# B and C of a state pair computed back to back on two halves of the array, the spline's scale moved into its clamps, and the planner's preference set to zero

## The chip, the cores and the metric

The kernel runs on one core of one Trainium2 chip. The metric is the device time of one execution in microseconds (us); three executions of the kernel before gave a median of 16343.33 us. One further execution was recorded by the hardware profiler; all views below are of that one.

## The reference

The input x has 32 images of 128 channels and 56 x 56 pixels, float32. Four residual layers follow each other, each on a group-normalised copy (`_gn`, 32 groups of 4 channels):

```python
x = x + _L0_conv_ref(_gn(x), ...)   # 1x1 conv with weights mixed per image, three dilated depthwise convs, SiLU
x = x + _L1_conv_ref(_gn(x), ...)   # cubic B-spline of every element
x = x + _L2_conv_ref(_gn(x), ...)   # linear attention over pooled keys, then a 3x3 depthwise conv
x = x + _L3_conv_ref(_gn(x), ...)   # Mamba layer over 3136 tokens
```

Two parts matter here. The spline layer clips the normalised element to -2..2 and sums ten cubic B-splines over 14 equidistant knots, with coefficients `coeffs`. The Mamba layer has 256 inner channels and 16 states a channel, and runs a recurrence over the 3136 tokens of an image:

```python
dA = jnp.exp(delta[..., None] * A)
dBu = delta[..., None] * B_ssm[:, :, None, :] * xc[..., None]
def step(h, inp):
    dA_t, dBu_t, C_t = inp
    h = dA_t * h + dBu_t
    y = jnp.einsum('bdn,bn->bd', h, C_t)
    return (h, y)
```

`delta`, `B_ssm` and `C_ssm` are projections of the same tokens, so B and C have 16 rows each for every token, shared by all 256 channels.

## The kernel before

**Tiling.** An image lies in on-chip memory as 128 channels x 3136 pixels and is worked in 7 chunks of 448 (`CH`, 8 rows of pixels). In the Mamba layer, a chunk is a `Scan` of 16 steps (`STEPS`): 8 pairs of states (`NPAIR`) times 2 halves of the channels (`DI`). One step covers 2 states x 128 channels, as two blocks of 64 channels x 2 states. There are 32 x 7 x 16 = 3584 steps, and the rest of the network is arranged around them.

**One scan step `n` of pair `p = n // 2`.** `b_rows` (line 1069) spreads the two B rows of the pair over 128 partitions by a matmul with a 0/1 matrix `sel` into the tile `pb`, which comes from a PSUM pool of a single buffer (`ps_bc`). `c_rows` (line 1060) does the same for C into a tile `mm` of the shared PSUM pool `ps_mm` of three buffers, and ScalarE copies it to `cb` (three buffers). Both happen only at the first of a pair's two steps and go through `both` (line 1054): B lies on rows 0 to 63 of `dbl`, C on rows 64 to 127, each with its low half of the bits 32 rows further on, so each matmul has 64 rows. `decay` (line 1076) makes two `da` tiles by Exp on ScalarE, into PSUM. `state` (line 1084) multiplies `du` by `pb` on VectorE into `h` and runs two scans with `da` over it. `products` (line 1100) multiplies `h` by `cb` on GpSimd into `hc`. `add` (line 1108) sums `hc` into the PSUM tile `y` by matmuls.

**The other work.** Beside the scan of image b run `until_scan` of image b+1 (spline, attention, first normalisation) and `first_layer` of image b+2 (the dynamic conv). Both are Python generators, called piece by piece from `images` (line 1196) so that their instructions are spread over the steps. `ssm_inputs` and `gate` prepare the next chunk's `delta`, `du`, `dbl` and `sz`.

**The spline** (line 747). Four lanes of 32 partitions hold the same 32 channels, each lane with another knot. For a chunk, ScalarE makes 12 hats `|a u + b|` (Abs, with the column `scl` as scale and a column of `bia` as bias) and, for each of four groups of channels, one Relu over three hats, `1 - |.|`. TensorE then sums the hats with weights `wspl`; squares, cubes and additions follow on ScalarE, VectorE and GpSimd. `scl` is 3.25/std of the channel (13 intervals over 4), `bia` is made of the knot's number and the mean.

**The order.** Nothing is issued as it is written. Each call becomes a `Work` with an engine, a modelled cost (`price`), the regions it reads and writes, a step and a value `ahead`; `plan.issue` then puts all works of a loop body into one order, and each engine executes its part of it strictly in that order. `plan.at(g, FIRST)` gives scan work of step g an `ahead` of 8, `SECOND` gives the next chunk's inputs 4, the rest has 0. A work is due at `(step - ahead) * 4.5` us, or earlier if a successor needs it. `attempt` (line 245) takes works one after the other in modelled time, at most 12 steps ahead of the oldest open one (`WINDOW`), each when its inputs and a buffer are there. Which of an engine's candidates is taken is decided here:

```python
late = at - self.PATIENCE[e] * (w.ahead > 0)
if w.table and w.table != table:
    late += 0.6
key = (max(late, free[e]), w.due, i)
```

`at` is when the work could start and `free` when the engine is free. With `PATIENCE` at 0.5 us, a scan work that can start up to 0.5 us after the engine is free counts as startable now, and if it is due earlier than other work that is ready, the engine is left idle for it. `plan.together(share)` joins the calls of a block into one work that is not split; its cost is the sum divided by `share` plus 0.1 us.

**Who calls what.** In `images`, step g calls `b_rows` for g+2, `state` g, `decay` g+1, `products` g, `c_rows` for g+`AHEAD` (2), `add` for g-2 and `store` for g-3.

Of the kernel before, what the change touches and what calls it, by code (L numbers as in the profile page):

```python
# [12 lines left out]
F32 = mybir.dt.float32  # L13
F32R = mybir.dt.float32r
AF = mybir.ActivationFunctionType
ALU = mybir.AluOpType
AX = mybir.AxisListType

P = 128
# [3 lines left out]
CH = ROWS * W  # L23
# [8 lines left out]
G = 32  # L32
NG = P // G
# [9 lines left out]
NKNOT = 14  # L43
# [11 lines left out]
DI = 2  # L55
# [11 lines left out]
NB = DI * P // Q  # L67
NPAIR = NST // 2
STEPS = NPAIR * DI
AHEAD = 2  # L70
LAG = 3
FIRST, SECOND = 8, 4
READY = 12
# [20 lines left out]
class Plan:  # L94
# [7 lines left out]
    TABLE = 1.28  # L102
    NEVER = 1e18
    GATE, BUSY = 3.413, 1.27
    PATIENCE = {"tensor": 0.5, "scalar": 0.5, "gpsimd": 0.3, "vector": 0.1, "sync": 0.0}

    def __init__(self, nc, tc):
        self.nc, self.tc = nc, tc
# [254 lines left out]
def tile_conv_stack(ctx: ExitStack, tc: tile.TileContext, out: bass.AP, x: bass.AP, w: dict):  # L363
# [150 lines left out]
    for s, knots in enumerate(KNOTS):  # L514
        for k, m in enumerate(knots):
            rows = slice(G * k, G * k + G)
            nc.vector.memset(kneg[rows, s : s + 1], -float(m))
            for i, (f, s1) in enumerate(SUMS):
                if s1 == s and (f == 2 or m % 2 == f):
                    nc.vector.tensor_copy(cs[rows, i : i + 1], (qc if f == 2 else py_)[rows, m - 1 : m])  # L520
# [61 lines left out]
    def psum(cols=CH, rows=P):  # L582
        t = ps_mm.tile([P, 512], F32, tag="mm", name="mm")
        return t[:rows, :cols]
# [161 lines left out]

    def spline(xt, st):
        mg, rs, ve, _ = group_stats(st)
        ab = small.tile([P, 2], F32, tag="ab", name="ab")

        kpu = (NKNOT - 1) / (GMAX - GMIN)
        nc.vector.tensor_scalar_mul(ab[:, 0:1], rs[:], kpu)
        nc.vector.tensor_mul(ab[:, 1:2], mg[:], ab[:, 0:1])
        nc.vector.tensor_scalar(ab[:, 1:2], ab[:, 1:2], -1.0, -GMIN * kpu, ALU.mult, ALU.add)

        top = small.tile([P, 1], F32, tag="top", name="top")
        nc.vector.tensor_mul(top[:], ve[:], rs[:])
        nc.scalar.activation(top[:], top[:], AF.Identity, bias=mg[:, 0:1], scale=GMAX)
        pab = psum(2 * NG)
        for c in range(NG):  # L760
            for k in range(4):
                nc.tensor.matmul(
                    pab[G * k : G * k + G, 2 * c : 2 * c + 2],
                    ident[:, G * c : G * c + G],
                    ab[:],
                    start=True,
                    stop=True,
                    tile_position=(0, G * k),
                )
        pab = pab.rearrange("p (c t) -> p c t", t=2)  # L770
        scl = small.tile([P, NG], F32, tag="scl", name="scl")
        nc.vector.tensor_copy(scl[:].unsqueeze(2), pab[:, :, 0:1])
        bia = small.tile([P, NG, 3], F32, tag="bia", name="bia")
        nc.vector.tensor_add(
            bia[:], kneg[:].unsqueeze(1).to_broadcast([P, NG, 3]), pab[:, :, 1:2].to_broadcast([P, NG, 3])
        )

        def load_u(j):

            t = stk.tile([P, NG, ROWS * PW], F32, tag="stack", name="stack")  # L780
            with plan.together():
                for k in range(4):
                    for c in range(NG):
                        nc.sync.dma_start(
                            t[G * k : G * k + G, c, 0:CH], xt[G * c : G * c + G, j * CH : (j + 1) * CH]
                        )
            return t

        us = [load_u(0)]
        after = Stats(xt)  # L790
        yield 6.0
        for j in range(NCH):
            if j + 1 < NCH:
                us.append(load_u(j + 1))
            u = us[j]
            xs = xt[:, j * CH : (j + 1) * CH]
            hats = wide.tile([P, NG, 3, CH], F32, tag="wide", name="hats")
            for c in range(NG):
                for s in range(3):
                    nc.scalar.activation(  # L800
                        hats[:, c, s, :], u[:, c, 0:CH], AF.Abs, bias=bia[:, c, s : s + 1], scale=scl[:, c : c + 1]
                    )
                nc.scalar.activation(hats[:, c], hats[:, c], AF.Relu, bias=one[:, 0:1], scale=-1.0)
                yield 3.6
            ind = tmp.tile([P, CH], F32, tag="v", name="ind")
            nc.gpsimd.tensor_scalar(ind[:], xs, top[:, 0:1], clast, ALU.is_ge, ALU.mult)

            def combined(f):
                ps = psum()
                mine = [i for i, (f1, _) in enumerate(SUMS) if f1 == f]  # L810
                for i in mine:
                    with plan.together(NG):
                        for c in range(NG):
                            nc.tensor.matmul(
                                ps[G * c : G * c + G, :],
                                wspl[:, i, :],
                                hats[:, c, SUMS[i][1], :],
                                start=(i == mine[0]),
                                stop=(i == mine[-1]),
                                tile_position=(0, G * c),  # L820
                            )
                return ps

            ps = combined(2)
            nc.vector.tensor_add(xs, xs, ps)
            nc.gpsimd.tensor_add(xs, xs, ind[:])
            after.take(j)
            yield 2.2
            for f in range(2):
                ps = combined(f)  # L830
                sq = tmp.tile([P, CH], F32, tag="v", name="sq")
                nc.scalar.activation(sq[:], ps, AF.Square)
                cube = tmp.tile([P, CH], F32, tag="v", name="cube")
                nc.vector.tensor_mul(cube[:], sq[:], ps)
                nc.gpsimd.tensor_add(xs, xs, cube[:])
                yield 1.7
        after.take(NCH)
        return after.st
# [202 lines left out]
    class Scan:  # L1041
# [15 lines left out]
            pair = sel[rows, 2 * p : 2 * p + 2, :].rearrange("p a b -> p (a b)")  # L1057
            nc.tensor.matmul(ps, pair, self.dbl[rows, :], start=True, stop=True)

        def c_rows(self, n):  # L1060

            p, db = divmod(n, DI)
            if db == 0:
                ps = psum()
                self.both(ps, C_ROW, p)
                self.cbs[p] = cbp.tile([P, CH], F32, tag="cb", name="cb")
                nc.scalar.copy(self.cbs[p][:], ps)

        def b_rows(self, n):

            p, db = divmod(n, DI)
            if db == 0:
                self.pbs[p] = ps_bc.tile([P, 512], F32, tag="bc", name="pb")[:, :CH]
                self.both(self.pbs[p], B_ROW, p)

        def decay(self, n):
            p, db = divmod(n, DI)
# [118 lines left out]
    def images(first, count, ahead):  # L1196
# [11 lines left out]
        def at(g, what):  # L1208

            if 0 <= g < count * NCH * STEPS:  # L1210
                getattr(scans[g // STEPS], what)(g % STEPS)
# [3 lines left out]
        for b in range(count):  # L1215
# [5 lines left out]
            for j in range(NCH):  # L1221
                k = b * NCH + j
                if k == 0:
                    last = new_last()
                    scans[0] = Scan(xt, image(ov, 0), last, 0)
                    for n in range(AHEAD):
                        at(n, "c_rows")
                    for n in range(2):
                        at(n, "b_rows")
                    at(0, "decay")  # L1230
                following = None
                if j + 1 < NCH:
# [5 lines left out]
                for n in range(STEPS):  # L1238
                    g = k * STEPS + n
                    plan.at(g)  # L1240
                    if n == 0 and j == NCH - 1:
                        rest.finish()
                    if n == READY:

                        following.finish()
                        gates.finish()
                        if j == NCH - 1:
                            layer0.finish()
                        if k + 1 < count * NCH:
                            nb, nj = divmod(k + 1, NCH)  # L1250
                            if nj == 0:
                                last = new_last()
                            scans[k + 1] = Scan(xts[nb % 3], image(ov, nb), last, k + 1)
                    plan.at(g, FIRST)
                    at(g + 2, "b_rows")
                    at(g, "state")
                    at(g + 1, "decay")
                    at(g, "products")
                    at(g + AHEAD, "c_rows")
                    at(g - LAG + 1, "add")  # L1260
                    at(g - LAG, "store")
                    plan.at(g, SECOND)
                    following.step(n)
                    if n >= READY - DI:
                        gates.step(n - READY + DI)
                    plan.at(g)
                    rest.step(j * STEPS + n)
                    if j * STEPS + n > LAG:
                        layer0.step(j * STEPS + n)
# [119 lines left out]
```

## Time and profile before

| what | value |
|---|---|
| three executions, us | 16294.26, 16343.33, 16363.43 |
| profiled execution: its own time, us | 16316.11 |
| profiled execution: span from first to last instruction, us | 16314.3 |
| mean granted TensorE clock, share of full speed | 0.893 |
| B matmul `pb<-dbl,sel`: count, mean ns | 1792, 512 |
| C matmul `mm<-dbl,sel`: count, mean ns | 1792, 502 |
| copy of C on ScalarE, `cb<-mm`: count, mean ns | 1792, 527 |
| decay `da`: count, mean ns | 7168, 633 |
| scan `h<-da,last,h`: count, mean ns | 6144, 1135 |
| `hc<-h,cb` on GpSimd: count, mean ns | 3584, 2092 |

How to read it: a busy time is the time in which an engine had an instruction in work; TensorE's are lengthened by its pipeline, so that the ends of two matmuls that follow each other overlap. An engine's idle time is put down to the instruction that released it last. All operations carry the line of a helper (338), which is why groups are told apart by the names of their tiles. The first 420 us are a prologue without a scan step; the last 400 us hold the scan of the last image alone, with the inputs of its own chunks.

### The profile page before, as it was taken

The numbers are of one execution on the slowest core, as the hardware profiler recorded it, in microseconds if no ns is written. First come the engines' busy times: TensorE is split into PE (matmuls) and PEld (weight loads), VectorE is DVE, ScalarE is ACT, GpSimd is POOL, SyncE is SP. The second block draws the span as 40 slices with busy tenths as digits, with TensorE's granted clock in tenths as the row PEclk, the third lists the DMA queues.
The fourth block names the chain that finished last, engine by engine and source line by source line (L and its number), as shares of the span: only waits on it lengthen the run. The fifth ranks groups of instructions, "written<-read, shape, count | busy, mean of one in ns | idle before, by whom it ended". The sixth has DMA issues, their size and how long they took to land. (4 is left out here: it accounts for less than half of the span.)

```text
span 16314.3 us, 212520 instructions
## 1 busy us (share of the span) xinstructions
PE 14202.3 (87%) x66400; PEld 4559.9 (28%) x66400; DVE 14306.2 (88%) x17314; ACT 11713.4 (72%) x21127; POOL 10785.0 (66%) x6406
## 2 busy tenths in 40 slices
PE   6888898888898888988888888888888898888887
PEld 2222222222222222222222222222222222222222
DVE  2898988989889898899988888888898898888889
ACT  3777777777677776777776777767777677776675
POOL 2676666666666666667666666666676666766666
PEclk7888998889998898998989988899988899888888
DMA  6344444344443444434444434444344444344421
GB/s 143 93 101 98 98 112 96 89 99 101 106 104 88 100 97 101 109 94 94 101 99 107 102 86 98 99 105 107 91 98 97 100 108 106 85 97 99 101 56 34
DMA packets 986159, 1589.93 MB, mean 97 GB/s; under 512 B 175622, under 2 KB 611209, under 8 KB 984331
## 3 DMA queue, kind: packets, MB, share of 16 engines
q1 hardware_dynamic: 985002, 1576.06, 41.0%
q8 instruction: 538, 8.81, 0.2%
q14 instruction: 619, 5.06, 0.1%
HBM read 785.62 MB, written 173.18 MB: 59 GB/s over the span
## 5 line engine op out<-in xcount | busy, mean ns | idle before, releaser
L338 POOL TENSOR_TENSOR hc<-h,cb 128x896 f32<-128x896 f32 x3584 | 7476.1, 2092 | 4173.5 <-DVE h L338 2178.7
L338 DVE TENSOR_TENSOR_SCAN h<-da,last,h 128x448 f32<-128x448 f32 x6144 | 6772.7, 1135 | 498.2 <-ACT da L338 451.3
L338 ACT ACTIVATE da<-delta,alog 128x448 f32<-128x448 f32 x7168 | 4481.8, 633 | 2635.3 <-DVE h L338 2369.4
L338 PE MATMUL y<-hc,sums 128*64 128x448 f32 x14336 | 3997.9, 638 | 625.6 <-POOL hc L338 617.8
L338 DVE TENSOR_TENSOR h<-du,pb 128x896 f32<-128x896 f32 x3584 | 3788.6, 1072 | 247.5 <-POOL hc L338 118.2
L338 PE MATMUL mm<-stack,dsT 96*32 96x448 f32 (+1 forms) x16128 | 1890.8, 575 | 59.4 <-DMA stack<-padded 16.8
L338 ACT ACTIVATE hats<-stack,bia,scl 128x448 f32<-128x448 f32 x2688 | 1887.6, 754 | 33.9 <-DVE bia L338 31.7
L338 PE MATMUL mm<-xn,winT 128*128 128x448 f32 x3584 | 1703.8, 590 | 39.8 <-ACT cb L338 13.5
L338 PEld LDWEIGHTS y<-hc,sums 128*64 128x64 f32 x14336 | 807.6, 147 | 2412.9 <-POOL hc L338 1436.9
L338 PE MATMUL mm<-hats,wspl 128*32 128x448 f32 x12544 | 1386.1, 563 | 33.3 <-ACT hats L338 30.4
L338 PE MATMUL pb<-dbl,sel 64*128 64x448 f32 x1792 | 918.3, 512 | 421.2 <-DVE h L338 364.3
L338 ACT ACTIVATE hats<-hats,one 128x1344 f32<-128x1344 f32 x896 | 1261.5, 1408 | 0.1
L338 ACT COPY cb<-mm 128x448 f32<-128x448 f32 x1792 | 940.3, 527 | 379.4 <-POOL hc L338 184.0
L338 PE MATMUL mm<-dbl,sel 64*128 64x448 f32 x1792 | 892.3, 502 | 363.5 <-DVE sz L338 63.7
L338 ACT ACTIVATE t<-mm 128x448 f32<-128x448 f32 x1568 | 829.2, 534 | 484.6 <-PE mm L338 480.3
L338 POOL TENSOR_TENSOR xt<-xt,g 128x448 f32<-128x448 f32 x672 | 767.5, 1142 | 524.1 <-DVE g L338 491.1
L338 DVE TENSOR_TENSOR_SCAN h<-da,h 128x448 f32<-128x448 f32 x1024 | 1054.1, 1070 | 28.3 <-ACT da L338 26.3
L338 PEld LDWEIGHTS mm<-xn,winT 128*128 128x128 f32 x3584 | 631.8, 197 | 986.0 <-issue 805.1
L338 DVE SCALAR_TENSOR_TENSOR g<-t,mm 128x448 f32<-128x448 f32 x672 | 407.7, 607 | 443.7 <-ACT t L338 392.8
L338 PEld LDWEIGHTS mm<-stack,dsT 96*32 96x32 f32 (+1 forms) x16128 | 445.2, 112 | 1156.3 <-issue 899.9
L338 PEld LDWEIGHTS mm<-dbl,sel 64*128 64x128 f32 x1792 | 351.2, 198 | 1453.5 <-issue 420.0
L338 PEld LDWEIGHTS pb<-dbl,sel 64*128 64x128 f32 x1792 | 358.6, 200 | 1419.1 <-issue 791.8
(187 smaller groups left out, 16166.2 us busy)
## 6 DMA issues: line engine op xcount, KB each, us to landing
stack<-padded SPq DMA_DIRECT2D x2688, 264.0 KB
stack<-xt SPq DMA_DIRECT2D x3584, 56.0 KB
delta<-delta SPq DMA_DIRECT2D x1792, 112.0 KB
du<-du SPq DMA_DIRECT2D x1792, 112.0 KB
padded<-yc SPq DMA_DIRECT2D x224, 264.0 KB
padded<-yc SPq DMA_DIRECT2D x256, 231.0 KB
xt<-x_dram SPq DMA_DIRECT2D x224, 224.0 KB
out_dram<-xt SPq DMA_DIRECT2D x224, 224.0 KB
```

Of the source, the lines that this page charges most:

```text
L338: call()
```

## The change

There are three edits.

1. `c_rows` and `b_rows` become one method `rows`: B and C of a pair are one work of two matmuls, B first, on rows 0 to 63 and 64 to 127 of the array. It is called for step g+`AHEAD` with `AHEAD` 3 in place of 2, and ahead of `state` in the list.

```diff
-AHEAD = 2
+AHEAD = 3
-        def c_rows(self, n):
-            p, db = divmod(n, DI)
-            if db == 0:
-                ps = psum()
-                self.both(ps, C_ROW, p)
-                self.cbs[p] = cbp.tile([P, CH], F32, tag="cb", name="cb")
-                nc.scalar.copy(self.cbs[p][:], ps)
-        def b_rows(self, n):
+        def rows(self, n):
             p, db = divmod(n, DI)
             if db == 0:
                 self.pbs[p] = ps_bc.tile([P, 512], F32, tag="bc", name="pb")[:, :CH]
-                self.both(self.pbs[p], B_ROW, p)
+                ps = psum()
+                with plan.together(2):
+                    self.both(self.pbs[p], B_ROW, p)
+                    self.both(ps, C_ROW, p)
+                self.cbs[p] = cbp.tile([P, CH], F32, tag="cb", name="cb")
+                nc.scalar.copy(self.cbs[p][:], ps)
...
-                    at(g + 2, "b_rows")
+                    at(g + AHEAD, "rows")
                     at(g, "state")
                     at(g + 1, "decay")
                     at(g, "products")
-                    at(g + AHEAD, "c_rows")
```

2. The spline's hats are left unscaled, `|u - mean - knot * std|`, so that Abs has a bias column only; the Relu `1 - (3.25/std) * |.|` gets the scale as a column in place of the constant -1. The small columns that feed them are computed accordingly.

```diff
-            nc.vector.memset(kneg[rows, s : s + 1], -float(m))
+            nc.vector.memset(kneg[rows, s : s + 1], -GMIN - m * (GMAX - GMIN) / (NKNOT - 1))
...
-        nc.vector.tensor_scalar_mul(ab[:, 0:1], rs[:], kpu)
-        nc.vector.tensor_mul(ab[:, 1:2], mg[:], ab[:, 0:1])
-        nc.vector.tensor_scalar(ab[:, 1:2], ab[:, 1:2], -1.0, -GMIN * kpu, ALU.mult, ALU.add)
+        nc.vector.tensor_scalar_mul(ab[:, 0:1], rs[:], -kpu)
+        nc.vector.tensor_mul(ab[:, 1:2], ve[:], rs[:])
+        nc.vector.tensor_scalar_mul(ab[:, 2:3], mg[:], -1.0)
...
-        nc.vector.tensor_mul(top[:], ve[:], rs[:])
...
-        nc.vector.tensor_add(
+        nc.vector.tensor_mul(
             bia[:], kneg[:].unsqueeze(1).to_broadcast([P, NG, 3]), pab[:, :, 1:2].to_broadcast([P, NG, 3])
         )
+        nc.vector.tensor_add(bia[:], bia[:], pab[:, :, 2:3].to_broadcast([P, NG, 3]))
...
-                        hats[:, c, s, :], u[:, c, 0:CH], AF.Abs, bias=bia[:, c, s : s + 1], scale=scl[:, c : c + 1]
+                        hats[:, c, s, :], u[:, c, 0:CH], AF.Abs, bias=bia[:, c, s : s + 1]
-                nc.scalar.activation(hats[:, c], hats[:, c], AF.Relu, bias=one[:, 0:1], scale=-1.0)
+                nc.scalar.activation(hats[:, c], hats[:, c], AF.Relu, bias=one[:, 0:1], scale=scl[:, c : c + 1])
```

3. The planner's preference for scan work is gone: an engine that is free takes what can start first, and the due time decides only between works that can start at the same time.

```diff
-    PATIENCE = {"tensor": 0.5, "scalar": 0.5, "gpsimd": 0.3, "vector": 0.1, "sync": 0.0}
+    PATIENCE = {"tensor": 0, "scalar": 0, "gpsimd": 0, "vector": 0, "sync": 0.0}
```

More of the change, by code (lines that the diff above doesn't have):

```diff
@@ L748, in spline @@
         mg, rs, ve, _ = group_stats(st)
-        ab = small.tile([P, 2], F32, tag="ab", name="ab")
+        ab = small.tile([P, 3], F32, tag="ab", name="ab")
         kpu = (NKNOT - 1) / (GMAX - GMIN)
-        nc.vector.tensor_scalar_mul(ab[:, 0:1], rs[:], kpu)
-        nc.vector.tensor_mul(ab[:, 1:2], mg[:], ab[:, 0:1])
-        nc.vector.tensor_scalar(ab[:, 1:2], ab[:, 1:2], -1.0, -GMIN * kpu, ALU.mult, ALU.add)
+        nc.vector.tensor_scalar_mul(ab[:, 0:1], rs[:], -kpu)
+        nc.vector.tensor_mul(ab[:, 1:2], ve[:], rs[:])
+        nc.vector.tensor_scalar_mul(ab[:, 2:3], mg[:], -1.0)
         top = small.tile([P, 1], F32, tag="top", name="top")
-        nc.vector.tensor_mul(top[:], ve[:], rs[:])
-        nc.scalar.activation(top[:], top[:], AF.Identity, bias=mg[:, 0:1], scale=GMAX)
-        pab = psum(2 * NG)
+        nc.scalar.activation(top[:], ab[:, 1:2], AF.Identity, bias=mg[:, 0:1], scale=GMAX)
+        pab = psum(3 * NG)
         for c in range(NG):
@@ L762, in spline @@
                 nc.tensor.matmul(
-                    pab[G * k : G * k + G, 2 * c : 2 * c + 2],
+                    pab[G * k : G * k + G, 3 * c : 3 * c + 3],
                     ident[:, G * c : G * c + G],
@@ L769, in spline @@
                 )
-        pab = pab.rearrange("p (c t) -> p c t", t=2)
+        pab = pab.rearrange("p (c t) -> p c t", t=3)
         scl = small.tile([P, NG], F32, tag="scl", name="scl")
@@ L1226, in images @@
                     for n in range(AHEAD):
-                        at(n, "c_rows")
-                    for n in range(2):
-                        at(n, "b_rows")
+                        at(n, "rows")
                     at(0, "decay")
```

## The prediction

> **What bounds the kernel now.** I read the busy shares first, then who waits for whom, then one image cut into stretches of eight scan steps, then single matmuls in the timeline. The page's first part:
>
> ```profile
> PE 14202.3 (87%) x66400; PEld 4559.9 (28%) x66400; DVE 14306.2 (88%) x17314; ACT 11713.4 (72%) x21127; POOL 10785.0 (66%) x6406
> ```
>
> Two engines are near full and none is full, so the shares alone name no bound. VectorE's waits, from the view of waits for that engine (us in total, times, longest):
>
> ```profile
> DVE h L338 <- ACT da L338: 478.9, 503, 3.0
> DVE g L338 <- ACT t L338: 392.8, 204, 17.0
> DVE xt L338 <- PE mm L338: 169.4, 83, 27.4
> DVE xc L338 <- ACT t L338: 121.5, 75, 15.5
> DVE sz L338 <- PE y L338: 97.3, 118, 3.7
> DVE h L338 <- PE pb L338: 88.7, 115, 1.9
> ```
>
> The scan waits for its decay 479 us in all; most of the rest goes back to a matmul (`t` is the Tanh of a matmul). `pb` itself ends only 89 us. One image, cut at every eighth step (stretch, length, busy us by engine, clock, DMA):
>
> ```profile
> core 0: us, PE busy (x) PEld busy (x) DVE busy (x) ACT busy (x) POOL busy (x), PEclk, DMA share, GB/s
> 5428.19:5456.60 28.41, 25.84 (x78) 8.72 (x79) 27.44 (x34) 14.95 (x32) 19.13 (x11) 1.00 0.18 47
> ...
> 5595.49:5629.03 33.54, 27.06 (x157) 8.13 (x155) 29.11 (x34) 33.08 (x57) 29.62 (x19) 1.00 0.50 116
> ...
> 5779.40:5820.19 40.79, 40.51 (x186) 12.19 (x186) 32.22 (x37) 21.87 (x46) 18.01 (x11) 0.99 0.46 115
> ```
>
> The bound changes with the stage. The first stretch belongs to VectorE (97% busy), the sixth to ScalarE (99%, the spline's hats), the eleventh to TensorE (99%, conv taps). Over 29 images cut at the same steps, ScalarE is busy 91, 97 and 91% in stretches 4, 6 and 8, where VectorE stands idle 13.7 us an image before scans; TensorE is 92 to 99% busy in stretches 5, 7, 9 and 11 to 13, where VectorE's share falls to 78% in stretch 11. So a saving on TensorE or ScalarE is worth its size in its own stretches and little elsewhere.
>
> **What the skill says.** Three places bear on this.
>
> - "TensorE: Matmul & The Clock Gate", Part 3, The mechanism: matmuls on different row groups run at once, starting about 4 ns apart. The trace agrees: B and C are already neighbours in 618 of the 1792 pairs (counted in the order of TensorE's matmuls), with starts 4 ns apart in the median. One of them, and one B alone:
>
> ```profile
> 5034.40 0.47 PE L338 MATMUL mm<-dbl,sel 64*128 64x448 f32 x1
> 5034.41 0.47 PE L338 MATMUL pb<-dbl,sel 64*128 64x448 f32 x1
> 5034.81 1.71 PE L338 MATMUL mm<-hats,wspl 128*32 128x448 f32 x16
> ...
> 5002.08 0.46 PE L338 MATMUL pb<-dbl,sel 64*128 64x448 f32 x1
> 5002.47 1.02 PE L338 MATMUL y<-xc,ddiag 128*128 128x448 f32 x2
> ```
>
> Both together hold TensorE 0.41 us, one alone 0.39: the second is free.
>
> - "TensorEngine Tiling (Array Packing)", Gotcha 1: two row tiles may not write one PSUM bank at the same time. `pb` and C's `mm` come from different pools and tiles of 512 floats, as they do in the 618 neighbours; no run here shows the forbidden case.
> - "ScalarE: Activation LUTs", What ACT_TABLE_LOAD costs: each per-partition column operand adds about 93 ns to an activation. The trace agrees: Square of 448 elements takes 532 ns without a column and 628 with a bias column, 96 ns more.
>
> **Part 1, the pair on TensorE.** Removed: for 1174 pairs (1792 - 618) a separate slot. A B alone holds TensorE 0.40 us at full clock (median over the 1174) and about 0.67 in throttled stretches; at the mean clock of 0.893 it is 0.40/0.893 = 0.45 us. So 1174 x 0.45 = 528 us of TensorE, 16.5 us an image. What of it is on the path: by stretch, the images have 2.0, 1.7, 2.0 and 3.2 separate pairs in stretches 5, 11, 12 and 13, with spacings of 0.40, 0.50, 0.50 and 0.42 us, so 0.8 + 0.8 + 1.0 + 1.3 = 3.9 us an image where TensorE sets the pace and VectorE has room. In stretches 7 and 9 VectorE is itself 97 to 98% busy, and elsewhere TensorE has idle time; I count those at nothing, since the idle time that TensorE already has hides them. 3.9 us x 32 = 125 us.
>
> The copy of C moves with its matmul. C now starts 4.1 us (median) ahead of B; afterwards with it. From B's start to the product that reads `cb` there are 9.8 us in the median and 4.5 at the 1% point; the matmul (0.47) and the copy (0.53) fit, so a later C costs nothing. `AHEAD` 3 lists the pair one step earlier, but `pb` has one buffer, so B still cannot start until the pair before has been multiplied.
>
> New condition: the pair, as one work, needs `pb`'s buffer and one of three `mm` buffers. Behind it in TensorE's queue stand the conv taps and the `y` sums; for its end waits `h`, which has from the end of the last multiplication to the next 4.2 us in the median, 3.0 at the quarter point and 2.0 at the 5% point. B needs some 0.6 of that. B is issued first, so a late `mm` buffer holds C and what is behind it, not B, except by the plan's order. From below it costs nothing, because a buffer usually frees within the window; from above, if every tenth pair lost 1 us, 179 us. I take the tight 5% twice over at 0.25 us: 1792 x 0.1 x 0.25 = 45, rounded to 40 us.
>
> **Part 2, the hats.** From the rows of the page:
>
> ```profile
> L338 ACT ACTIVATE hats<-stack,bia,scl 128x448 f32<-128x448 f32 x2688 | 1887.6, 754 | 33.9 <-DVE bia L338 31.7
> L338 ACT ACTIVATE hats<-hats,one 128x1344 f32<-128x1344 f32 x896 | 1261.5, 1408 | 0.1
> ```
>
> 2688 x 96 ns = 258 us less, 896 x 96 = 86 more, net 172 us of ScalarE, 5.4 us an image. Stretches 4, 6 and 8 hold 32 of the 84 hats and 9 or 10 of the 28 Relus of an image: (32 - 9.5) x 0.096 = 2.2 us there. The works of neighbouring stretches can slide into the gap, as the spline is a chain through all eight stretches; I take 2.8 us, between 2.2 and 5.4, x 32 = 90 us. The small columns: six VectorE operations an image before, six after; three columns in place of two in the small matmuls (191 ns each) change nothing visible. Cost 0, with up to 32 x 0.3 = 10 us if the chain were bare.
>
> **Part 3, the preference.** No instruction goes or comes; the order changes. While an engine has spare work, the plan no longer holds it idle for up to 0.5 us. Where ScalarE or TensorE set the pace that is a gain, where VectorE does, a loss: a decay can find a Relu just begun. A decay starts when a scan has freed its `da` buffer and is needed after the other scan (1.14) and a multiplication (1.07), so it has 2.2 - 0.63 = 1.6 us less the hand-overs; a Relu of 1.41 + 0.10 = 1.5 us just uses that up. In the timeline, 184 of the 896 Relus are directly ahead of a decay that a scan waited for, 227 us in all (1.23 us each). Bounds: all 896 would cost 875 us; all 184 gone would gain 227. I take 25 more such cases, 30 us of loss, no gain elsewhere.
>
> **Sum.** -125 + 40 - 90 + 30 = -145 us on the span of 16314: 16169. Outside the span lie 1.8 us (16316.11 - 16314.3), so 16171 for an execution like the profiled one. The median of the three runs is 27 us above the profiled execution; taken half into account, since the three spread over 69 us, that is 16185 us, 1.0% less. What is late next: in stretches 11 to 13 still the conv taps, in 4 to 8 still the hats.
>
> **Rivals.**
>
> - *More than its own stretches.* The 16.5 us an image of TensorE also shorten the Tanh and `y` waits outside the full stretches, and ScalarE's 5.4 count in full. If two thirds of both arrive, 14.6 x 32 = 467 us: 15875 us. For it: VectorE waits over 800 us for things that begin with a matmul. Against it: stretches 1, 3, 7 and 9 are VectorE's own.
> - *Hidden anyway.* Both savings turn into idle time, and 40 + 30 of losses stand against 70 or so of gains: 16330 us. For it: `pb` ends only 89 us of waits. Against it: 99% of TensorE in stretch 11.
> - *Slower: Relus ahead of decays.* Without the preference ScalarE begins a 1.5 us Relu whenever no decay is ready at that instant, and the scan stalls 1.23 us. It decides from (215 - 40) / 1.23 = 142 additional cases; at 320 more, half of all Relus stalled, it is +394 - 175 = +219 us: 16550 us. For it: the Relu is the longest activation of the spline and grows, and it already ends half of the waits for `da`. Against it: in those stretches ScalarE sets the pace, and idle time planned there is lost as well.
> - *No overlap.* Against it stand the 618 pairs; I give it nothing.
>
> **Chances.** The forecast 0.45, more than its stretches 0.13, hidden 0.15, slower 0.27. A change within 0.5% (82 us) cannot be told from none here. Faster by more: 0.45 + 0.13 = 0.58; within: 0.15; slower: 0.27. Range: the forecast's own, from the bounds of `pb`'s buffers (0 to 179), of the hats (70 to 172) and of the first part (125 to 260), is 16030 to 16260. For 8 in 10 it goes down to 15930, into the first rival, and up to 16500, short of the slower case's centre.
>
> **What would show it.** Right: `pb` and C start within some 10 ns in nearly all of 1792 pairs; mean of hats 660 ns and of Relu 1500; TensorE's busy time lower by some 400 to 530 us; stretches 11 to 13 together shorter by 3 us or more an image. Wrong: VectorE's wait for `da` clearly over 479 us, with Relus ahead of it; its wait for `pb` over 130 us; or the stretches that were VectorE's own grown. Since the plan orders everything anew, a change of order in stretches that none of the edits touches would also break the sum.

## The result and the profile after

The changed kernel takes 16455.49 us (median of five runs, 16448.56 to 16468.55) against 16343.33 before: 1.0072 times as long, with a 95% interval of 1.0054 to 1.0091. The forecast was 16185 us. The profiled execution took 16458.47 us, its span was 16456.7.

The parts of the page that answer to those shown of before:

```profile
span 16456.7 us, 212542 instructions
PE 13957.8 (85%) x66400; PEld 4387.0 (27%) x66400; DVE 14323.9 (87%) x17314; ACT 11541.4 (70%) x21127; POOL 10779.7 (66%) x6406
```

The work did shrink. TensorE is busy 244 us less, where the prediction looked for 400 to 530, and ScalarE 172 us less. That this is the prediction's own figure is partly luck: the hats' two groups are busy 143 us less (664 and 1505 ns for one Abs and one Relu), and the rest comes from other work. VectorE works about as long as before (+18 us) and waits longer. The view of waits of VectorE in the changed kernel (us in total, times, longest):

```profile
DVE h L338 <- ACT da L338: 470.4, 409, 10.0
DVE h L338 <- POOL hc L338: 208.3, 196, 3.5
DVE g L338 <- ACT t L338: 202.2, 158, 16.9
...
DVE h L338 <- PE mm L338: 154.7, 129, 2.9
...
DVE h L338 <- PE pb L338: 44.4, 48, 2.9
```

Two lines of the same view before, which the prediction did not show:

```profile
DVE h L338 <- POOL hc L338: 118.2, 93, 3.0
...
DVE h L338 <- PE mm L338: 9.9, 16, 1.0
```

Three things are new in it. The wait for `da` is as long in total as before, but its longest is 10.0 us, not 3.0. `h` waits for `mm`, which is C's matmul directly behind B's, 155 us where it was 10 before; with `pb` that is 199 against 99 us. And it waits 208 us for `hc`, where it was 118. The wait of `g` for the Tanh is what fell, from 393 to 202 us.

The pair itself does what it should. One from TensorE's timeline:

```profile
2005.71 0.46 PE L338 MATMUL pb<-dbl,sel 64*128 64x448 f32 x1
2005.71 0.46 PE L338 MATMUL mm<-dbl,sel 64*128 64x448 f32 x1
2006.10 0.38 PE L338 MATMUL mm<-mv,gmat 128*128 128x1 f32 x2
```

Both start in the same hundredth, and 0.39 us later TensorE is on. In the order of TensorE's matmuls, B and C are neighbours in 1767 of 1792 pairs (618 before), 3 ns apart in the median.

Where the time went can be read from the starts of VectorE's multiplications `h<-du,pb`, cut at every eighth step as in the prediction (means of 29 images; one trace of each kernel). Stretches 11 to 13 together are 8.3 us an image shorter, and 5 and 9 together 5.4 us. But stretches 1, 2, 3, 10 and 14 together are 18.0 us longer. The first and the third, in which VectorE is 97% busy or more in the kernel before, grow by 2.7 and 2.9 us: this is one of the signs that the prediction named for being wrong.

The long waits for `da` have one picture. ScalarE and VectorE in the changed kernel, from the timeline (start, length, what; in brackets VectorE's idle time and what ended it):

```profile
1057.43 1.51 ACT L338 ACTIVATE hats<-hats,one,scl 128x1344 f32<-128x1344 f32 x1
1058.83 1.23 ACT L338 ACTIVATE hats<-stack,bia 128x448 f32<-128x448 f32 x2
1059.94 0.64 ACT L338 ACTIVATE yc<-mm,aggb 128x448 f32<-128x448 f32 x1
1060.46 1.51 ACT L338 ACTIVATE hats<-hats,one,scl 128x1344 f32<-128x1344 f32 x1
1061.86 0.53 ACT L338 COPY cb<-mm 128x448 f32<-128x448 f32 x1
1062.40 1.28 ACT L338 ACT_TABLE_LOAD   x1
1063.69 0.58 ACT L338 ACTIVATE rstd<-rstd 128x448 f32<-128x448 f32 x1
1064.18 1.18 ACT L338 ACTIVATE da<-delta,alog 128x448 f32<-128x448 f32 x2
```

```profile
1055.23 0.63 DVE L338 BATCH_NORM_STATS2 st<-xt 128x6 f32<-128x448 f32 x1
1064.83 2.19 DVE L338 TENSOR_TENSOR_SCAN h<-da,last,h 128x448 f32<-128x448 f32 x2 [8.97 <-ACT da L338]
```

ScalarE is not idle. It works off a run of hats, then loads the activation table, and only then makes the Exps that the scan has waited for since 1056. Earlier it had run a Ln, which needs another table than Exp. From ScalarE's order I cut out every stretch from the end of the last Ln to the load of the table for Exp. In the loop and after, 254 such stretches lie in each kernel. Before, the longest is 1.4 us and no hat lies in one; in the changed kernel 15 are over 5 us long and 240 hats lie in them. These stretches, with the load and the first Exp, hold 210 us of VectorE's idle time before and 348 after, which is 138 of the 142 us that the span grew. That looks like a whole explanation. The experiments show that it is not: without these stretches the changed kernel is no faster.

### The profile page after: what moved, and what is told of

Read it like the earlier page. It is cut to its first block, busy times and chain, and to the rows that moved or that the text cites. A ratio compares the mean times of both kernels' runs of the same rounds, so it can differ in the third digit from the quotient of the medians.

```text
span 16456.7 us, 212542 instructions
## 1 busy us (share of the span) xinstructions
PE 13957.8 (85%) x66400; PEld 4387.0 (27%) x66400; DVE 14323.9 (87%) x17314; ACT 11541.4 (70%) x21127; POOL 10779.7 (66%) x6406
## 5 line engine op out<-in xcount | busy, mean ns | idle before, releaser
L338 DVE TENSOR_TENSOR h<-du,pb 128x896 f32<-128x896 f32 x3584 | 3781.3, 1072 | 508.0 <-POOL hc L338 208.3
L338 PE MATMUL mm<-stack,dsT 96*32 96x448 f32 (+1 forms) x16128 | 1981.9, 597 | 81.0 <-ACT cb L338 21.4
L338 ACT ACTIVATE hats<-stack,bia 128x448 f32<-128x448 f32 x2688 | 1658.1, 664 | 7.0 <-PE mm L338 3.8
L338 PE MATMUL mm<-hats,wspl 128*32 128x448 f32 x12544 | 1485.4, 595 | 169.5 <-ACT cb L338 49.3
L338 ACT ACTIVATE hats<-hats,one,scl 128x1344 f32<-128x1344 f32 x896 | 1348.1, 1505 | 1.1
L338 PE MATMUL mm<-dbl,sel 64*128 64x448 f32 x1792 | 937.3, 523 | 155.4 <-ACT yc L338 41.7
L338 PEld LDWEIGHTS mm<-hats,wspl 128*32 128x32 f32 x12544 | 374.1, 117 | 1136.7 <-issue 611.9
L338 ACT ACT_TABLE_LOAD x512 | 656.9, 1283 | 28.4 <-DVE sz L338 20.0
```

Source lines behind the costliest of these rows:

```text
L338: call()
```

## The experiments

In the labels, P stands for the preference at zero, S for the hats, R for the pair with `AHEAD` 3. "No penalty" means that a penalty which the plan puts on work with another activation table is taken from scan and input work (explained below). All ratios are to the kernel before, with their 95% intervals. "Long" counts stretches of over 5 us after a Ln; the next two columns split VectorE's idle time after the first 430 us (gaps over 0.15 us) into what lies in stretches after a Ln, with load and first Exp, and the rest.

| run | what it has | median us | ratio | interval | long | idle there, us | idle elsewhere, us |
|---|---|---|---|---|---|---|---|
| before | | 16343.33 | 1 | | 0 | 210 | 1390 |
| changed | R S P | 16455.49 | 1.0072 | 1.0054 to 1.0091 | 15 | 348 | 1392 |
| e_P | P | 16497.19 | 1.0096 | 1.0080 to 1.0111 | 37 | 680 | 1102 |
| e_S | S | 16571.89 | 1.0145 | 1.0130 to 1.0161 | 20 | 400 | 1389 |
| e_R | R | 17289.69 | 1.0582 | 1.0568 to 1.0597 | 30 | 578 | 1894 |
| e_RS | R S | 17237.39 | 1.0550 | 1.0536 to 1.0564 | 30 | 553 | 1938 |
| e_SP | S P | 16064.50 | 0.9840 | 0.9824 to 0.9855 | 1 | 191 | 1155 |
| f_0 | no penalty | 16859.22 | 1.0315 | 1.0301 to 1.0329 | 0 | 230 | 1839 |
| f_P | P, no penalty | 16308.69 | 0.9984 | 0.9978 to 0.9991 | 0 | 234 | 1315 |
| f_R | R, no penalty | 17130.40 | 1.0482 | 1.0468 to 1.0497 | 5 | 387 | 1898 |
| f_RSP | R S P, no penalty | 16505.97 | 1.0101 | 1.0085 to 1.0116 | 0 | 218 | 1444 |
| f_SP | S P, no penalty | 16135.31 | 0.9884 | 0.9866 to 0.9902 | 0 | 212 | 1135 |
| u_RSP | R S P, two works | 16444.13 | 1.0072 | 1.0056 to 1.0088 | 26 | 474 | 1165 |
| f_USP | as f_RSP, two works | 16522.99 | 1.0119 | 1.0100 to 1.0138 | 0 | 227 | 1479 |
| f_R2SP | as f_RSP, `AHEAD` 2 | 16448.80 | 1.0077 | 1.0063 to 1.0091 | 0 | 262 | 1441 |
| f_A3SP | f_SP, C three ahead | 16499.16 | 1.0099 | 1.0083 to 1.0114 | 0 | 251 | 1472 |
| e_Sfix | hats, order of before | 16299.32 | 0.9976 | 0.9969 to 0.9983 | 0 | 225 | 1369 |
| n_RSP | changed, no overlap | 16796.03 | 1.0281 | 1.0267 to 1.0295 | 15 | 360 | 1683 |
| b_L19 | before, landing 1.9 | 16287.82 | 0.9975 | 0.9964 to 0.9985 | 0 | 183 | 1390 |
| a_L19 | changed, landing 1.9 | 16467.70 | 1.0082 | 1.0068 to 1.0096 | 20 | 431 | 1388 |

**One part at a time.** Theory A laid the loss on the preference, B on the pair, C on the new order as such.

```diff
-    PATIENCE = {"tensor": 0.5, "scalar": 0.5, "gpsimd": 0.3, "vector": 0.1, "sync": 0.0}
+    PATIENCE = {"tensor": 0, "scalar": 0, "gpsimd": 0, "vector": 0, "sync": 0.0}
```

e_P, this edit alone:

> The kernel before with the preference alone set to zero (pairs and hats as before). Theory A, the preference is the loss: its removal costs more than the whole change, about 1.015 to 1.025 times before, and the other two parts gain. Theory B, the pair is the loss: 0.995 to 1.003. Theory C, any new order moves the time by some per cent in either sense and parts don't add: anything within 0.99 to 1.015, unrelated to the sum of the others.

e_S, the spline's edit alone:

> The kernel before with the spline's scale in the clamps alone. 172 us less of ScalarE. Theories A and B: 0.992 to 0.997 times before (90 us or so, as the prediction had it). Theory C: may come out slower than before although it only takes work away.

e_R, the pair and `AHEAD` 3 alone:

> The kernel before with the pair of matmuls and AHEAD 3 alone, preference and hats as before. Theory A: 0.988 to 0.995 (TensorE's 528 us show). Theory B: 1.008 to 1.02, with VectorE waiting for pb or for the mm buffers. Theory C: within 0.99 to 1.015, not explained by either.

e_RS, everything but the preference:

> The changed kernel with the preference put back to 0.5, 0.5, 0.3 and 0.1. Theory A: 0.985 to 0.993 times before, faster than both kernels. Theory B: 1.003 to 1.015, about as slow as the changed kernel. Theory C: no more than a new draw, within 0.99 to 1.015.

Each part alone is slower, and the parts don't add: 1.0, 1.5 and 5.8% against 0.7% for all three. Theory A falls, since the kernel with the preference put back (e_RS) is 5.5% slower than before. B's sign holds but not its size, and not by the wait that it named: in e_R `h` waits 110 us for the pair where it waited 99 before, and it is VectorE's idle time before other work than `h` that grows, from 893 to 1491 us. The column of long stretches shows what the parts have in common: all four kernels have 20 to 37 of them where before had none. So theory D was added: the plan's handling of tables makes the long waits. The plan adds 0.6 us to the start of a work whose table isn't the loaded one. After a Ln, an Exp thus always looks later than a hat, which needs no table and is ready, so the hats go first for as long as any is ready. Which order happens to put a run of hats behind a Ln was not looked into.

**The penalty taken from scan and input work.**

```diff
-                    if w.table and w.table != table:
+                    if w.table and w.table != table and not w.ahead:
                         late += 0.6
```

f_0, the kernel before with it:

> Kernel before, with the planner's table penalty of 0.6 us taken from scan and input work (it stays for work with ahead 0). The kernel before has no hats behind a Ln that hold back a table load. Theory D (long stalls, up to 20 us, where the plan lets the run of hats go ahead of the Exp after a Ln): 0.995 to 1.005 times before. Theory C (any new order costs some per cent): 1.005 to 1.02.

f_P, the preference at zero with it:

> Preference set to zero, with the same edit of the penalty. e_P had 37 stretches of over 5 us between the last Ln and the next table load, with 525 us of VectorE's idle time in them, and 288 us less idle time than before outside of them. Theory D: 0.98 to 0.992 times before. Theory A (the preference itself is the loss): 1.008 or more. Theory C: 1.0 to 1.015.

f_R, the pair with it:

> The pair and AHEAD 3 alone, with the same edit of the penalty. Theory D alone: the whole 5.8% goes, 0.995 to 1.005 times before. Theory B (the pair itself costs): about 424 us of stalls go and some 500 us stay, 1.025 to 1.035.

f_RSP, the changed kernel with it:

> The changed kernel with the same edit of the penalty. It had 15 long stretches with 195 us of VectorE's idle time. Theory D: about 0.993 to 1.0 times before, 195 us or so faster than the changed kernel. Theory B alone: 1.005 to 1.01, as the changed kernel.

The edit takes the long stretches away (0, 0, 5 and 0 are left), and with the preference at zero the time falls as D said in direction, from 16497 (e_P) to 16309 us (f_P), though not to the 0.992 or less that it expected. But f_R keeps 4.8% of its 5.8%, f_RSP is no faster than the changed kernel, and f_0 loses 3.2% though before had no long stretch to lose, more than either theory expected. D is a true part and not the cause of the result. f_0 also shows that a rule of the plan can move the time by 3% with the same work.

**Same order, other durations.** These two separate the work saved from the order. Both keep the order of every engine as it was; only operands differ.

e_Sfix, the kernel before with the hats' durations of the change:

```diff
-                        hats[:, c, s, :], u[:, c, 0:CH], AF.Abs, bias=bia[:, c, s : s + 1], scale=scl[:, c : c + 1]
+                        hats[:, c, s, :], u[:, c, 0:CH], AF.Abs, bias=bia[:, c, s : s + 1]
-                nc.scalar.activation(hats[:, c], hats[:, c], AF.Relu, bias=one[:, 0:1], scale=-1.0)
+                nc.scalar.activation(hats[:, c], hats[:, c], AF.Relu, bias=one[:, 0:1], scale=scl[:, c : c + 1])
```

> The kernel before in exactly its own order (the hats' modelled costs are kept as they were), with the scale dropped from the Abs and put on the Relu, so that the durations are those of the change; the hats' values are not the spline's (the columns are the old ones). It measures what 172 us less of ScalarE are worth where the order stays. If the sum of the prediction holds for this part: 0.993 to 0.996 times before. If the time is set by the order and VectorE's chain: 0.998 to 1.001.

n_RSP, the changed kernel without the overlap:

```diff
-            rows = slice(row, row + 2 * LOW)
+            rows = slice(0, P) if row else slice(0, C_ROW)
```

> The changed kernel in exactly its own order, but C's matmul takes all 128 rows of the array in place of 64, so that it cannot run beside B (cb then holds B + C in place of C). It measures what the overlap of the pair is worth where the order stays. If TensorE's 528 us are worth a quarter, as predicted: 1.008 to 1.01 times the changed kernel, 1.015 to 1.018 times before. If they are hidden: within 0.3% of the changed kernel.

The hats of e_Sfix, in its groups of ScalarE (count, busy us, mean ns, idle time before them):

```profile
L338 ACT ACTIVATE hats<-stack,bia 128x448 f32<-128x448 f32 x2688 | 1637.6, 660 | 36.2 <-DVE bia L338 31.8 <-PE mm L338 4.4
L338 ACT ACTIVATE hats<-hats,one,scl 128x1344 f32<-128x1344 f32 x896 | 1343.5, 1499 | 0.1
```

The durations are as forecast, 94 ns less and 91 more; 168 us of the hats' busy time go, and the time falls by 33 us (16331.90, the median of before in its group, less 16299.32). The interval of the ratio gives 28 to 51 us. So between a sixth and a third of the saved time reaches the end, between the two ranges that the run's expectation named.

n_RSP takes 341 us more than the changed kernel (16796.03 - 16455.49), 2.1%. A part of its timeline shows B and C now behind each other, each with its own slot:

```profile
2010.69 0.74 PE L338 MATMUL pb<-dbl,sel 64*128 64x448 f32 x1
2011.36 0.74 PE L338 MATMUL mm<-dbl,sel 128*128 128x448 f32 x1
2012.78 1.86 PE L338 MATMUL mm<-xn,wzT 128*128 128x448 f32 x2 [0.68 <-ACT cb L338]
```

This takes the overlap from all 1792 pairs, while the prediction's 125 us were for the 1174 that stood apart before. At the same rate these 1174 come to 223 us (an estimate), still 1.8 times the prediction. Cut into stretches as above, n_RSP is 9.8 us an image longer than the changed kernel, 0.3 to 1.2 in every one of the fourteen stretches. Only 2.6 of that lie in stretches 5 and 11 to 13, where the prediction had counted. So the overlap gains, and what makes the changed kernel slower has to be sought in its order.

**A neutral disturbance.** One constant of the plan that has nothing to do with the change:

```diff
-    RATE, LANDING = 2e5, 1.8
+    RATE, LANDING = 2e5, 1.9
```

b_L19, before:

> The kernel before with one constant of the planner moved, a DMA's landing modelled as 1.9 us in place of 1.8: the same work, another order. Theory C (the order before is a good draw, any other costs): 1.01 to 1.04 times before. Otherwise 0.998 to 1.003.

a_L19, the changed kernel:

> The changed kernel with the same constant moved to 1.9 us. Theory C: within 1% of the changed kernel to either side, and not slower than b_L19 by as much as the changed kernel is slower than before. If the change itself costs 0.7%: slower than b_L19 by about that.

Both orders change in thousands of places, and the times by 0.3% and 0.1%. The gap between the two stays, 1.1% here. Theory C in its strong form, that any new order costs, is out. This one small shift left the times nearly where they were; the changed rule of f_0 did not.

**The pair undone, and its halves.** Theory E laid the loss on the coupling: B has to wait for `pb`'s buffer and a buffer of `mm` at once.

e_SP, the changed kernel with B and C as before:

> The changed kernel with the pair undone (B and C as before, AHEAD 2), hats and preference as changed. Theory E (the pair as one work has to wait for pb's buffer and a buffer of mm at once, and that waiting eats what the overlap brings): 0.985 to 1.0 times before, so faster than the changed kernel by 0.7% or more. If the pair brings a net gain: slower than the changed kernel by up to 2%.

u_RSP, the changed kernel with the pair as two works:

```diff
-                with plan.together(2):
-                    self.both(self.pbs[p], B_ROW, p)
-                    self.both(ps, C_ROW, p)
+                self.both(self.pbs[p], B_ROW, p)
+                self.both(ps, C_ROW, p)
```

> The changed kernel with B and C listed as two works in place of one (AHEAD 3 for both, no together). Theory E: B is free again of the buffers of mm, so VectorE's wait for pb and mm before h goes from some 200 us to under 110, at the price of a part of the overlap; near e_SP, and faster than the changed kernel unless long stretches with the table of Ln grow (it has more of them, so up to 200 us more idle time there). If AHEAD 3 is the cost: as slow as the changed kernel outside of those stretches.

f_SP, as e_SP without the penalty:

> Hats and preference as changed, B and C as before, and no table penalty for scan and input work. No long stretches with the table of Ln are left. Theory E: 0.99 to 1.0 times before, and 0.8 to 1.5% faster than f_RSP, from which it differs by the pair alone.

f_USP, as u_RSP without the penalty:

> As f_RSP, but B and C as two works. It differs from f_RSP in the coupling alone. Theory E: faster than f_RSP by 0.5 to 1.3%, close to f_SP. If the new order as such or AHEAD 3 is the cost: within 0.3% of f_RSP.

e_SP is the fastest kernel of the study, 1.6% faster than before. Its page and three of VectorE's waits:

```profile
PE 14144.2 (88%) x66400; PEld 4545.5 (28%) x66400; DVE 14311.2 (89%) x17314; ACT 11545.5 (72%) x21127; POOL 10780.7 (67%) x6406
```

```profile
DVE h L338 <- ACT da L338: 327.8, 441, 10.9
...
DVE h L338 <- PE pb L338: 71.4, 94, 1.9
...
DVE h L338 <- POOL hc L338: 63.1, 76, 1.7
```

`h` waits 151 us less for `da` than before and a third as long for `hc` as in the changed kernel. The pair on top costs 16455.49 - 16064.50 = 391 us. VectorE's idle time grows by 157 us after a Ln (348 - 191) and by 237 us elsewhere (1392 - 1155). By what `h` waits for, it grows by 123 us for the pair (199 against 76, the 71.4 for `pb` and 4.6 for `mm`), by 143 for the decays (470.4 - 327.8) and by 145 for the products `hc` (208.3 - 63.1), and shrinks by some 20 before all other work together.

That the pair's part is the loss is shown, and not in this one setting only. It costs 946 us alone, 666 with the hats, 391 with hats and preference, 271 without the penalty (f_R less f_0) and 371 with hats and preference and no penalty (f_RSP less f_SP).

That it is the coupling is not shown. In u_RSP the idle time elsewhere falls to 1165 us, e_SP's value, as E expected, and `h` waits 3 us for `mm`; but the long stretches grow to 26, and the time stays. In f_USP, with no long stretch, it does not fall at all: 1479 us. These two runs do not move the coupling alone, as f_USP's expectation had it. Listed as two works, B and C are neighbours in only 382 (u_RSP) and 568 (f_USP) of the 1792 pairs, against 1781 in f_RSP. So f_USP gives up most of the overlap too, which by n_RSP's 0.19 us a pair would be worth some 230 us (1213 x 0.19, an estimate), and still takes as long as f_RSP. That leaves room for a cost of the coupling of that size.

Two more runs start from f_SP.

f_R2SP, the coupled pair at two steps ahead:

> f_RSP with AHEAD 2 in place of 3: the coupled pair, listed one step later. f_SP (no pair, 2) took 0.988 times before, f_RSP (pair, 3) 1.010, f_USP (two works, 3) 1.012. Theory E (coupling): near f_RSP, 1.005 to 1.012. Theory G (listing the rows three steps ahead is the cost, with or without coupling): near f_SP or, with the overlap, faster, 0.975 to 0.99.

f_A3SP, C alone at three steps ahead, not coupled (`AHEAD = 3` in the code of before):

> f_SP with AHEAD 3 for C alone: B stays at two steps ahead, the two are not coupled. Theory G in the form that an early C holds the buffers of mm and cb: 1.005 to 1.012, like f_USP. If B's early listing or its place is the cost: 0.985 to 0.992, like f_SP.

Either costs about as much as both together: 16449 and 16499 us, from 16135, where f_RSP takes 16506. VectorE's waits before `h`, for its decay and for B and C, in f_SP, f_R2SP and f_A3SP:

```profile
DVE h L338 <- ACT da L338: 340.3, 387, 3.9
...
DVE h L338 <- PE pb L338: 49.5, 67, 2.0
```

```profile
DVE h L338 <- ACT da L338: 394.9, 450, 4.5
...
DVE h L338 <- PE mm L338: 194.6, 219, 2.9
```

```profile
DVE h L338 <- ACT da L338: 492.6, 307, 6.6
...
DVE h L338 <- PE pb L338: 162.1, 145, 1.7
```

With the coupling, `h` waits 244 us for the pair (194.6 for `mm`, and 49.7 for `pb`) where f_SP has 52: 192 of 356 us of added idle time. That is what E expected, though f_R2SP also moves the pair to another place in the list. With C early and free, `h` waits 164 us for B, 112 more than in f_SP, though B itself was not touched, and 152 us more for decays.

The two look unlike on TensorE. In f_R2SP, with 1723 pairs as neighbours, it is busy 392 us less than in f_SP; in f_A3SP only 296 pairs are neighbours, where f_SP has 654, and it is busy 296 us more. A part of f_A3SP's loss can thus be overlap that it lost, some 70 us at 0.19 us a pair (an estimate). What they share shows in the waits of ScalarE, in front of the copy of C. Its wait for TensorE in f_SP, f_R2SP and f_A3SP:

```profile
ACT cb L338 <- PE mm L338: 86.5, 67, 3.1
```

```profile
ACT cb L338 <- PE mm L338: 732.7, 565, 6.8
```

```profile
ACT cb L338 <- PE mm L338: 247.8, 221, 3.4
```

With its waits for a free `cb` and for others, ScalarE stands idle in front of this copy for 257 us in f_SP, 825 in f_R2SP and 500 in f_A3SP; in e_SP it is 160, in the changed kernel 983. The copy stands in the same queue as the decays, so they cannot pass it. No run tests whether this is the cause: ScalarE is busy only 70% of the time, and VectorE is itself idle during 209 of the 983 us, 184 of the 825 and 134 of the 500.

## Why the prediction was wrong

**The step that failed** is the pair's term in part 1, -125 + 40 = -85 us, where 391 us more were measured on the hats and preference of the change. In its last paragraph I priced what the new condition costs at 40 us, "from above, if every tenth pair lost 1 us, 179 us", and in the paragraph ahead of it "a later C costs nothing". The direct wait lay within my bound: C starts more than 1 us behind B in 73 of the 1792 pairs, 172 us in all, and `h` waits 123 us more for the pair than in e_SP. What the sum had nothing for is the rest, 143 us more for decays and 145 more for products. I priced a wait of one instruction for one buffer. The edit moved B and C relative to all other work, and the list of every engine was drawn up anew. Against the overlap's gain, what I had booked at 40 us then comes to some 610 us (391 + 223; the two are measured in different orders, so it is an estimate).

The other two parts missed the other way. Hats and preference together gain 279 us (16343.33 - 16064.50), where the sum had -90 + 30 = -60. So the terms were further off than the total, 112 us slower in place of 145 faster.

**The overlap.** Its mechanism was right: starts within nanoseconds, 1767 pairs. I counted it only in stretches where TensorE is full, and it was worth 1.8 times that: three quarters of what n_RSP loses lie in the other stretches, booked at nothing. "A later C costs nothing" looked at the product on GpSimd alone, with its 9.8 us from B. It left out ScalarE, which makes the copy: its wait for C's matmul in front of `cb` is 842 us in the changed kernel, 162 before and 28 in e_SP. How much of that reaches the end is not measured.

**The hats.** Their saving of time on ScalarE was right where the order stays (168 us in e_Sfix, 172 forecast). Its worth there is 33 us, not 90. My 2.2 to 5.4 us an image were a share of busy time in full stretches. That VectorE's chain there gives back most of it is my reading and is not shown.

**The preference.** Booked as 30 us of loss, "no gain elsewhere". Against e_S it is worth -507 us (16064.50 - 16571.89), against e_RS -782 (16455.49 - 17237.39), against before alone +157 (of its own group, 16497.19 - 16340.18). Outside the stretches after a Ln it lowers VectorE's idle time against before and against e_S, by 288 and 234 us, and with the preference alone the long stretches turn this into a loss, which is gone in f_P. The slower rival, hats before decays, named the right engine and the right neighbours. It saw a single Relu and 1.23 us; the runs show whole runs of hats behind a Ln, up to 10 us of waiting in the changed kernel. They go when the table penalty goes, which stood in the printed code and which I did not price. It isn't what makes the changed kernel slower than before, though: f_RSP, without them, is not faster. That its 16550 us lie nearer to the measured time than the forecast does owes more to luck than to its mechanism.

**The range.** The bounds that I named for it, added up at their ends, reach from about 15930 to 16340 us and not from 16030 to 16260.

**Additivity** is what the sum rested on, and it does not hold here: P and S alone cost 1.0 and 1.5%, together they gain 1.6%.

**Open.** Which step of the order turns a pair, or an early C, into 300 us and more of waits is not settled. A buffer of `mm` kept for C, which would test the coupling alone, and the old place in the list for the pair were not tried (all eight banks of PSUM are in use). Neither was ScalarE's copy moved behind the decays. The granted clock fell as well, from 0.893 to 0.881. It is not enough to sort the kernels: f_P at 0.882 is as fast as before, and u_RSP at 0.889 as slow as the changed kernel. But no run separates what a lower clock costs from what lowers it.

## What to carry to other kernels

Where a planner draws up the order, as here, an edit of one work's cost, place or buffers is a new program for every engine; price the saved work by a run at the old order, and the new order by itself. Binding a work with a tight due time to a freely movable one is not free because the second has slack: the tight one can inherit the other's waits (244 us in f_R2SP, 52 in f_SP), and the loose one loses its place. And look at a long stall for what the waiting engine's supplier was doing: here it was busy with hats and had a table switch behind them, and a change of the plan's rule took these stalls away.

## What the runs showed of the hardware

Two 64-row matmuls on different halves of the array together hold it as long as one, 0.39 us to the next start, and at a fixed order the missing overlap cost 341 us in 1792 pairs, 0.19 us a pair (n_RSP). Taking a per-partition scale from 448-element activations saved 94 ns each and adding one to 1344-element activations cost 91 ns, so the column's price was about the same at both lengths. A table load took 1283 ns, but the wait around it reached 10 us, because other work stood ahead of the load. And the same instructions in another order, with one rule of the plan changed, took 3.2% longer at a mean TensorE clock of 0.868 in place of 0.893.
